# The hand-over from layer 1's attention to a 30-step recurrence: row factors through DRAM, two PSUM banks kept open, parameters made earlier

## The chip, the cores and the metric

The kernel runs on one core of one Trainium2 chip. TensorE (PE) multiplies matrices and transposes tiles, VectorE (DVE) and ScalarE (ACT) work element by element, GpSimd (POOL) does some elementwise work and issues gathers and scatters, SyncE (SP) issues transfers. The metric is the device time in microseconds (us) of the whole launch; lower is better.

## The reference, cut to what matters

Two layers work on 3327 nodes with 256 features. Each layer is a graph attention over a 0/1 adjacency matrix, then a feed-forward part. In layer 0 that part is a mixture of 16 experts, two for each node. In layer 1 it is a recurrence of 30 steps, each a small elementwise update, a layer norm and a 256x256 product. All is fp32.

```python
# layer 1, attention; x comes in layer-normed
wh = h @ W
wh1 = wh @ a[:F_OUT, :]
wh2 = wh @ a[F_OUT:, :]
e = wh1 + wh2.T
e = jnp.where(e > 0, e, ALPHA * e)
e = jnp.where(adj > 0, e, NEG_BIG)
attention = jax.nn.softmax(e, axis=-1)
h_prime = attention @ wh
return jax.nn.elu(h_prime)
...
# layer 1, recurrence: 30 times
h = h + 0.01 * jnp.tanh(h)
h = h * jax.nn.sigmoid(h)
h = _layernorm(h, ln_w, ln_b)
h = jnp.einsum('bsc,dc->bsd', h, W) + b
```

## The kernel before

The nodes stand in 26 tiles of 128 rows (NT = 26). The state x stays on chip. The program is written in one piece for all engines; a planner orders each engine's instructions by what they depend on and by when it expects them to be ready, so that an instruction can run well before its place in the text. An instruction handed to `keep_in_program_order` is held behind the instruction that was written before it for the same engine. Tiles come from pools: a pool with `bufs=2` gives each tile name two slots in turn, and pools that are closed make room for later ones. PSUM, where TensorE writes, has 8 banks of 512 fp32 in each of 128 partitions.

**Experts** (`work_off`, L797). 61 turns follow one another. A turn takes 128 gathered tokens through one expert's three matrices: products at L786 and L827, with weights that SP loads (L769 to L771) some turns ahead. PSUM banks come from `bank()`, a pool of four. Between the turns other pieces are slipped in by turn number: layer 1's parameters are loaded at turn 16 (L805), two preparations of the attention's weights come at turns 22 and 26 (L807, L809).

**Layer 1's attention** (`attend`, L201). Destination tiles are taken in nine parts, eight of three tiles and a last of two (`groups2`; its tiles are 24 and 25). For each part there are 26 steps j over source tiles. In a step ScalarE makes e (L252) from `rb`, VectorE makes the masked weights pT (L257), and TensorE adds to one accumulator for each destination tile (L262, 257 columns). `rb` holds the part's row factors: the vector `sc.row` of each of its tiles, laid along the free axis and repeated in every partition. `row_factors` (L214) makes it with one fp32 matmul for each tile (L221, two records each in the trace) into a PSUM bank of pool ps2, and ScalarE copies the bank (L225). The text asks for the next part's factors at step 13. When a part is done, VectorE reads its accumulators (L235 and L943 to L947, tile by tile), SP writes the result to DRAM (`kept`, L951), and VectorE normalizes the rows in place (L127); these pieces are mixed in among the next part's steps.

Two PSUM pools are open during the attention: ps2 with two slots named "bank", and ps2o with two slots for each of acc0, acc1 and acc2, six banks. Before the attention the same accumulators serve a projection; `spot` (L918) deals them out by a counter that starts at 0. Behind the attention stand the recurrence's parameters (L960 to L973): bb, a row vector, and wc, the 256x256 matrix with the layer norm's weight and mean worked in. They take four fp32 matmuls (eight records) and eight VectorE instructions.

**Recurrence** (L976 to L1046). The 26 tiles form seven groups, six of four and one of two. 30 steps of seven groups are taken in order, two groups to a pair, so that in 14 groups, two steps, seven pairs come: mostly 4+4, once 4+2 and once 2+4. For both groups of a pair `turn_group` (L992) runs first: tanh (L998), a sum on GpSimd (L1000), silu (L1001), statistics (L1005) and transposes into `pt` (L1008, two for each tile). Then `next_state` (L1012) runs for both: ScalarE copies `pt` to `zT` (L1019), in two pieces for the first group of a pair and in one for the second; TensorE multiplies by wc into `po` (L1024, two records for each matmul, 256 columns); VectorE scales and shifts into x (L1030). Transposes and products are held in program order. `pt` and `po` have two banks each and two slots each, eight banks, in pools ps3t and ps3o, which are opened when ps2 and ps2o are closed.

Of the kernel before, what the change touches and what calls it, by code (L numbers as in the profile page):

```python
# [20 lines left out]
P = 128  # L21
# [4 lines left out]
G = 4  # L26
# [4 lines left out]
def gat_moe_gat_recurrent_ffn(ctx: ExitStack, tc: tile.TileContext, a: dict, out: bass.AP):  # L31
# [169 lines left out]
    def attend(sc, wh, heads, row_groups, per_bank, finish, finished, pools, later, leave=False):  # L201
# [11 lines left out]

        def row_factors(ts, h):  # L214

            rb = rows_p.tile([P, most * P], F32, name="rb")
            for c0 in range(0, len(ts), 4):
# [25 lines left out]
        for k, (ts, h) in enumerate(parts):  # L243
# [4 lines left out]
            for j in range(NT):  # L248
                if j == NT // 2 and k + 1 < len(parts):
                    following = row_factors(*parts[k + 1])  # L250
# [107 lines left out]
    with ExitStack() as moe:  # L358
# [413 lines left out]

        def features_first(row):
# [23 lines left out]
        def work_off(s0, s1, aside):  # L797
# [3 lines left out]
            for s in range(s0, s1 + 1):  # L801
# [6 lines left out]
                if s == FIRST + 10:  # L808
                    without_mean(wv1, D + 2, ones_r, bank())  # L809
                hidT = made  # L810
# [80 lines left out]
    steps = ctx.enter_context(tc.tile_pool(name="steps", bufs=2))  # L891
    with ExitStack() as st:
# [7 lines left out]
        ps = st.enter_context(tc.tile_pool(name="ps2", bufs=2, space=PSUM))  # L900
# [15 lines left out]
        count = 0  # L916
# [39 lines left out]
        attend(sc, wh, 1, groups2, 1, add_elu, begin_state, (run, rows_p, ps, ps_o), deque())  # L956

        pb = ps.tile([P, 512], F32, name="bank")[:, :D]  # L960
        for k in range(KD):
            nc.tensor.matmul(
                pb, lhsT=lb[:, k : k + 1].to_broadcast([P, P]), rhs=fW[:, k, :], start=(k == 0), stop=(k == KD - 1)
            )
        nc.vector.tensor_tensor(bb, pb, fb, ALU.add)
        nc.vector.tensor_scalar(bb, bb, S, None, op0=ALU.mult)
        pc = ps.tile([P, 512], F32, name="bank")[:, :D]
        for k in range(KD):
            nc.vector.tensor_scalar(wc[:, k, :], fW[:, k, :], lw[:, k : k + 1], None, op0=ALU.mult)
            nc.tensor.matmul(pc, lhsT=ones_r, rhs=wc[:, k, :], start=(k == 0), stop=(k == KD - 1))  # L970
        for k in range(KD):
            nc.vector.scalar_tensor_tensor(wc[:, k, :], pc, -1.0 / D, wc[:, k, :], op0=ALU.mult, op1=ALU.add)
            nc.vector.tensor_scalar(wc[:, k, :], wc[:, k, :], S, None, op0=ALU.mult)  # L973


    with ExitStack() as st:  # L976
# [66 lines left out]
        for i in range(0, len(parts), 2):  # L1043
            two = [part + turn_group(part[1]) for part in parts[i : i + 2]]
            for part, pieces in zip(two, (2, 1)):
                next_state(*part, pieces)  # L1046
# [49 lines left out]
```

The softmax here doesn't subtract the row's maximum and nothing guards it: scores larger than these inputs give would overflow.

## Time and profile before

| what | us |
|---|---|
| three timed runs | 1965.48, 1968.25, 1968.59 (median 1968.25) |
| the profiled execution | 1964.56 |
| its span, first to last instruction | 1962.6 |
| layer 1's attention, first L262 to its last | 792.10 to 1091.83 |
| first transposes of the recurrence | 1094.32 |
| first L1024, last L1024's end | 1097.73, near 1955.5 |

A group's line in the profile names the line of the kernel, the engine, the operation and output<-input. "[2.49 <-DVE high L944]" at the end of a line says how long the engine was idle before it, and whose result ended that. Matmul ends are modelled, and some matmul records are missing, so idle time of TensorE is best read from starts. The chain of waits follows the last instruction back to what released it. SPq is SP's queue of transfers.

### The profile page before, as it was taken

Reading aid. Unit: us, or ns where it says so; the run is one execution under the profiler, and the core shown is the slowest. Engines: PE = TensorE matmul, PEld = TensorE weight load, DVE = VectorE, ACT = ScalarE, POOL = GpSimd, SP = SyncE. Lnnn points to the kernel's source line nnn. Section 1 sums busy time; section 2 is a strip of 40 time slices with the busy share of each in tenths; the row PEclk is TensorE's granted clock in tenths of the full one; section 3 lists DMA queues with packets and bytes.
Section 4 is the critical chain, followed back from the end, with each engine's and each line's share of the span. In section 5 each row is a group of like instructions: output and inputs, shape, how many; then the busy total and the mean of one; then the engine's idle time right before and its main releaser. Section 6 shows DMA issues by size and latency. Waiting matters only on the chain.

```text
span 1962.6 us, 33704 instructions
## 1 busy us (share of the span) xinstructions
PE 1908.9 (97%) x12032; PEld 1747.3 (89%) x12032; DVE 1281.6 (65%) x3827; ACT 1096.5 (56%) x1509; POOL 936.5 (48%) x864
## 2 busy tenths in 40 slices
PE   7999999999999997999999999999999999999998
PEld 6999999998999995888888888888888888888887
DVE  6887788832222225566767777777777777777778
ACT  2977766721111113666555666666666666666664
POOL 3020202353333322010000488878888887888886
PEclk9999999999999998999999999999999999999999
DMA  8978051099999874000000000000000000000003
GB/s 168 117 104 118 6 86 50 18 307 303 357 326 336 280 245 148 2 15 9 17 9 17 28 1 1 1 1 1 1 1 1 1 1 1 1 1 1 1 1 118
DMA packets 139756, 157.09 MB, mean 80 GB/s; under 512 B 52028, under 2 KB 99365, under 8 KB 139587
## 3 DMA queue, kind: packets, MB, share of 16 engines
q1 hardware_dynamic: 123466, 122.05, 20.1%
q0 software_dynamic: 11440, 28.09, 8.3%
q10 hardware_dynamic: 4680, 4.76, 0.7%
q8 instruction: 98, 1.61, 0.3%
q14 instruction: 72, 0.58, 0.1%
HBM read 164.58 MB, written 29.78 MB: 99 GB/s over the span
## 4 chain that ended last, share of the span: by engine, by line
PE 71%; issue 9%; POOL 5%; DVE 4%; DMA 3%; ACT 1%; SPq 0%; POOLq 0%; DVEq 0%; ACTq 0%
PE po L1024 35%; PE acc L262 24%; PE pt L1008 8%; POOL given L831 2%; DVE pT L257 2%; POOL rb L730 2%; DMA given<-wh,to 2%; PE bank L786 1%; PE bank L499 1%; DMA wh<-in_w_dram 1%; DMA lists<-pair,ati 1%; DVE x L913 1%; PE bank L221 0%; PE acc L162 0%; ACT zT L1019 0%
## 5 line engine op out<-in xcount | busy, mean ns | idle before, releaser
L1024 PE MATMUL po<-wc,zT 128*128 128x256 f32 x3120 | 700.3, 382 | 3.6 <-ACT zT L1019 3.6
L1024 PEld LDWEIGHTS po<-wc,zT 128*128 128x128 f32 x3120 | 583.0, 190 | 89.0 <-ACT zT L1019 11.2
L1000 POOL TENSOR_TENSOR th<-th,x 128x1024 f32<-128x1024 f32 (+1 forms) x210 | 460.8, 2216 | 120.7 <-ACT th L998 117.9
L252 ACT ACTIVATE e<-rb,minus,full 128x384 f32<-128x384 f32 (+3 forms) x494 | 400.5, 824 | 180.1 <-DVE pT L257 164.1
L257 DVE SCALAR_TENSOR_TENSOR pT<-e,part,adjT 128x384 f32<-128x384 f32 (+3 forms) x494 | 380.5, 774 | 137.5 <-PE acc L262 117.0
L1005 DVE BATCH_NORM_STATS2 stats<-z 128x6 f32<-128x256 f32 x780 | 275.1, 413 | 168.5 <-ACT z L1001 168.5
L1019 ACT COPY zT<-pt 128x512 f32<-128x512 f32 (+1 forms) x300 | 196.7, 721 | 294.1 <-PE pt L1008 294.1
L1030 DVE SCALAR_TENSOR_TENSOR x<-po,rr,bb 128x256 f32<-128x256 f32 x780 | 323.2, 475 | 48.7 <-PE po L1024 42.7
L262 PE MATMUL acc<-wh,pT 128*128 128x129 f32 x2704 | 310.1, 276 | 1.6 <-DVE pT L257 1.6
L262 PEld LDWEIGHTS acc<-wh,pT 128*128 128x128 f32 x2704 | 305.2, 192 | 2.0 <-DVE pT L257 2.0
L262 PE MATMUL acc<-s_wh,pT 128*128 128x257 f32 x1352 | 295.3, 380 | 0.8 <-DVE pT L257 0.7
L262 PEld LDWEIGHTS acc<-s_wh,pT 128*128 128x128 f32 x1352 | 255.9, 190 | 37.7 <-DVE pT L257 1.8
L120 POOL TENSOR_TENSOR rstd<-ve,neg_half 128x4 f32<-128x4 f32 (+3 forms) x28 | 30.4, 1086 | 415.1 <-DVE ve L118 331.5
L989 POOL TENSOR_TENSOR rr<-rr,neg_half 128x4 f32<-128x4 f32 (+1 forms) x210 | 207.2, 989 | 15.0
L1001 ACT ACTIVATE z<-th 128x1024 f32<-128x1024 f32 (+1 forms) x210 | 201.6, 1011 | 0.6 <-POOL th L1000 0.5
L998 ACT ACTIVATE th<-x 128x1024 f32<-128x1024 f32 (+1 forms) x210 | 198.4, 1002 | 0.9 <-DVE x L127 0.9
L1008 PE MATMUL pt<-ident,z 128*128 128x128 f32 x1560 | 189.1, 274 | 2.5 <-DVE high L944 2.5
L1008 PEld LDWEIGHTS pt<-ident,z 128*128 128x128 f32 x1560 | 178.6, 142 | 13.3 <-issue 2.9
L786 PEld LDWEIGHTS bank<-hT,wh 128*128 128x128 f32 x1280 | 149.1, 192 | 5.7 <-issue 3.7
L786 PE MATMUL bank<-hT,wh 128*128 128x128 f32 x1280 | 150.1, 275 | 3.4 <-DMA wh<-in_w_dram 3.4
L820 DVE TENSOR_TENSOR pT<-e,bank 128x512 f32<-128x512 f32 x61 | 41.9, 687 | 165.2 <-PE bank L786 165.1
L816 ACT ACTIVATE e<-bank 128x512 f32<-128x512 f32 x61 | 36.4, 597 | 196.7 <-PE bank L786 184.4
(189 smaller groups left out, 1333.5 us busy)
## 6 DMA issues: line engine op xcount, KB each, us to landing
wh<-in_w_dram SPq DMA_DIRECT2D x120, 512.0 KB
first_set<-in_w_dram SPq DMA_DIRECT2D x63, 512.0 KB
in_bytes<-in_adj_dram POOLq DMA_DIRECT2D x3, 2496.0 KB, 28.7
x<-in_x_dram SPq DMA_DIRECT2D x6, 512.0 KB
kept<-x SPq DMA_DIRECT2D x8, 384.0 KB
old<-kept SPq DMA_DIRECT2D x6, 512.0 KB
out_dram<-x SPq DMA_DIRECT2D x6, 512.0 KB
table_x<-row ACTq DMA_DIRECT2D x3, 768.0 KB
```

Of the source, the lines that this page charges most:

```text
L252: nc.scalar.activation(e[:, : n * P], rb[:, : n * P], AF.Relu, scale=sc.full[:, j, h : h + 1], bias=sc.minus[:, j, h : h + 1],)
L257: masked = nc.vector.scalar_tensor_tensor(pT[:, : n * P], e[:, : n * P], sc.part[:, j, h : h + 1], adjT[:, j // 2, ts[0] * P : (ts[-1] + 1 ...
L262: nc.tensor.matmul(po[c], lhsT=pT[:, c * P : (c + 1) * P], rhs=wh[:, j, h, :], start=(j == 0 and c % per_bank == 0), stop=(j == NT - 1), s ...
L786: nc.tensor.matmul(p[:, f, :], lhsT=w[:, k, f * P : (f + 1) * P], rhs=hT[:, k, :], start=(k == 0), stop=(k == KD - 1),)
L989: nc.gpsimd.tensor_tensor(r[:, :n], r[:, :n], neg_half[:, :n], ALU.pow)
L998: nc.scalar.activation(th[:, :n, :], hs, AF.Tanh, scale=1.0 / S)
L1000: nc.gpsimd.tensor_tensor(th[:, :n, :], th[:, :n, :], hs, ALU.add)
L1001: nc.scalar.activation(z[:, :n, :], th[:, :n, :], AF.Silu, scale=1.0 / S)
L1005: nc.vector.bn_stats(stats[:, j, :], z[:, j, :])
L1008: nc.tensor.transpose(pt[:, j, k, :], z[:, j, k * P : (k + 1) * P], ident)
L1024: nc.tensor.matmul(po[:, j, :], lhsT=zT[:, j, k, :], rhs=wc[:, k, :], start=(k == 0), stop=(k == KD - 1),)
L1030: nc.vector.scalar_tensor_tensor(x[:, ts[0] + j, :], po[:, j, :], rr[:, j : j + 1], bb, op0=ALU.mult, op1=ALU.add)
```

## The change

Four things change.

1. In layer 1's attention the row factors of all parts but the first are read from DRAM. At step 2 of the first part `put_factors` transposes `sc.row` once (26 rows of 128), VectorE copies that to SBUF, and SP writes it to a DRAM tile. `row_factors` then issues a read on SP that repeats the part's rows in all 128 partitions.
2. The pool ps2 is opened outside the attention's scope and stays open through the recurrence. `turn_group` takes its banks in turn from ps2 and from ps3t; each bank holds the transposes of two tiles, and `next_state` copies each bank by itself, for both groups of a pair. ps3t so has two banks instead of four.
3. The recurrence's parameters are made in the experts, at turn 30.
4. The counter of `spot` starts at 1, so that the accumulators' names are first used in the order acc2, acc0, acc1.

```diff
...
     quick = []
-    def attend(sc, wh, heads, row_groups, per_bank, finish, finished, pools, later, leave=False):
+    def attend(sc, wh, heads, row_groups, per_bank, finish, finished, pools, later, leave=False, spread=None):
...
         most = max(len(ts) for ts in row_groups)
         parts = [(ts, h) for ts in row_groups for h in range(heads)]
+        if spread:
+            queue, room = spread
+            factors = dram.tile([NT * heads, P], F32, name=f"factors{heads}")
+        def put_factors():
+            p = ps_r.tile([P, 512], F32, name="bank")[: NT * heads, :P]
+            nc.tensor.transpose(p, sc.row.rearrange("p t h -> p (t h)"), ident)
+            lines = room()[: NT * heads, :P]
+            nc.vector.tensor_copy(lines, p)
+            queue.dma_start(factors, lines)
         def row_factors(ts, h):
             rb = rows_p.tile([P, most * P], F32, name="rb")
+            if spread and (ts, h) != parts[0]:
+                here = factors[ts[0] * heads + h : ts[0] * heads + h + 1, :]
+                queue.dma_start(
+                    rb[:, : len(ts) * P].rearrange("p (c q) -> p c q", q=P),
+                    bass.AP(tensor=here.tensor, offset=here.offset, ap=[[0, P], [heads * P, len(ts)], [1, P]]),
+                )
+                return rb
             for c0 in range(0, len(ts), 4):
                 some = ts[c0 : c0 + 4]
                 p = ps_r.tile([P, 4, P], F32, name="bank")
...
             acc = [ps_o.tile([P, 512], F32, name=f"acc{q}") for q in range((n + per_bank - 1) // per_bank)]
             po = [acc[c // per_bank][:, (c % per_bank) * W : (c % per_bank + 1) * W] for c in range(n)]
             for j in range(NT):
+                if spread and j == 2 and k == 0:
+                    put_factors()
                 if j == NT // 2 and k + 1 < len(parts):
                     following = row_factors(*parts[k + 1])
                 e = work.tile([P, most * P], F32, name="e")
...
             nc.sync.dma_start(w2, a["w2"][bass.ds(e, 1)].rearrange("e (k p) h -> p (e k) h", p=P), **kw)
             behind = nc.sync.dma_start(w3, a["w3"][bass.ds(e, 1)].rearrange("e (f p) o -> p (e f) o", p=P), **kw).ins
+        def recurrence_parameters():
+            pb = bank()[:, :D]
+            for k in range(KD):
+                nc.tensor.matmul(
+                    pb, lhsT=lb[:, k : k + 1].to_broadcast([P, P]), rhs=fW[:, k, :], start=(k == 0), stop=(k == KD - 1)
+                )
+            nc.vector.tensor_tensor(bb, pb, fb, ALU.add)
+            nc.vector.tensor_scalar(bb, bb, S, None, op0=ALU.mult)
+            pc = bank()[:, :D]
+            for k in range(KD):
+                nc.vector.tensor_scalar(wc[:, k, :], fW[:, k, :], lw[:, k : k + 1], None, op0=ALU.mult)
+                nc.tensor.matmul(pc, lhsT=ones_r, rhs=wc[:, k, :], start=(k == 0), stop=(k == KD - 1))
+            for k in range(KD):
+                nc.vector.scalar_tensor_tensor(wc[:, k, :], pc, -1.0 / D, wc[:, k, :], op0=ALU.mult, op1=ALU.add)
+                nc.vector.tensor_scalar(wc[:, k, :], wc[:, k, :], S, None, op0=ALU.mult)
         def features_first(row):
             pt = ps_o.tile([P, 512], F32, name="acc0")[:, :D].rearrange("p (k q) -> p k q", k=KD)
             hT = turn.tile([P, 2, KD, P], F32, name="hT")[:, 0]
...
                     score_vectors()
                 if s == FIRST + 10:
                     without_mean(wv1, D + 2, ones_r, bank())
+                if s == FIRST + 14:
+                    recurrence_parameters()
                 hidT = made
                 if s < s1:
                     if s + 4 < s1:
...
     kept = dram.tile([NP, D], F32, name="kept")
     steps = ctx.enter_context(tc.tile_pool(name="steps", bufs=2))
+    ps = ctx.enter_context(tc.tile_pool(name="ps2", bufs=2, space=PSUM))
     with ExitStack() as st:
         keep = st.enter_context(tc.tile_pool(name="keep2", bufs=1))
...
         sc = Scores(keep, 1, s_wh[:, :, 0, 0:2].rearrange("p t (s h) -> p t s h", h=1))
         nc.vector.memset(wh[:, :, :, D : D + 1], 1.0)
         work = st.enter_context(tc.tile_pool(name="work2", bufs=2))
-        ps = st.enter_context(tc.tile_pool(name="ps2", bufs=2, space=PSUM))
         ps_o = st.enter_context(tc.tile_pool(name="ps2o", bufs=2, space=PSUM))
         names = cycle(("th", "z", "zT"))
...
                     nc.vector.tensor_tensor(here, here, two[k], ALU.add)
         add_results(groups1[:3])
-        count = 0
+        count = 1
         def spot():
             nonlocal count
...
             tiles = [x[:, t, :] for t in ts]
             normalized(tiles, tiles, S)
-        attend(sc, wh, 1, groups2, 1, add_elu, begin_state, (run, rows_p, ps, ps_o), deque())
-        pb = ps.tile([P, 512], F32, name="bank")[:, :D]
-        for k in range(KD):
-            nc.tensor.matmul(
-                pb, lhsT=lb[:, k : k + 1].to_broadcast([P, P]), rhs=fW[:, k, :], start=(k == 0), stop=(k == KD - 1)
-            )
-        nc.vector.tensor_tensor(bb, pb, fb, ALU.add)
-        nc.vector.tensor_scalar(bb, bb, S, None, op0=ALU.mult)
-        pc = ps.tile([P, 512], F32, name="bank")[:, :D]
-        for k in range(KD):
-            nc.vector.tensor_scalar(wc[:, k, :], fW[:, k, :], lw[:, k : k + 1], None, op0=ALU.mult)
-            nc.tensor.matmul(pc, lhsT=ones_r, rhs=wc[:, k, :], start=(k == 0), stop=(k == KD - 1))
-        for k in range(KD):
-            nc.vector.scalar_tensor_tensor(wc[:, k, :], pc, -1.0 / D, wc[:, k, :], op0=ALU.mult, op1=ALU.add)
-            nc.vector.tensor_scalar(wc[:, k, :], wc[:, k, :], S, None, op0=ALU.mult)
+        attend(
+            sc, wh, 1, groups2, 1, add_elu, begin_state, (run, rows_p, ps, ps_o), deque(),
+            spread=(nc.sync, lambda: fin.tile([P, D], F32, name="low")),
+        )
     with ExitStack() as st:
         ps_t = st.enter_context(tc.tile_pool(name="ps3t", bufs=2, space=PSUM))
+        turns = cycle((ps, ps_t))
         ps_o = st.enter_context(tc.tile_pool(name="ps3o", bufs=2, space=PSUM))
         last_p = st.enter_context(tc.tile_pool(name="last", bufs=2))
...
             nc.gpsimd.tensor_tensor(th[:, :n, :], th[:, :n, :], hs, ALU.add)
             nc.scalar.activation(z[:, :n, :], th[:, :n, :], AF.Silu, scale=1.0 / S)
             stats = small.tile([P, G, 6], F32, name="stats")
-            pt = ps_t.tile([P, G, KD, P], F32, name="pt")
+            pool = next(turns)
+            pt = [pool.tile([P, 2, KD, P], F32, name="bank") for _ in range(0, n, 2)]
             for j in range(n):
                 nc.vector.bn_stats(stats[:, j, :], z[:, j, :])
                 for k in range(KD):
                     tc.keep_in_program_order(
-                        nc.tensor.transpose(pt[:, j, k, :], z[:, j, k * P : (k + 1) * P], ident)
+                        nc.tensor.transpose(pt[j // 2][:, j % 2, k, :], z[:, j, k * P : (k + 1) * P], ident)
                     )
             return pt, stats
-        def next_state(step, ts, pt, stats, pieces):
+        def next_state(step, ts, pt, stats):
             n = len(ts)
             hs = x[:, ts[0] : ts[0] + n, :]
             rr = inv_norm(stats, n)
             zT = steps.tile([P, G, KD, P], F32, name="zT")
-            for c in range(0, n, G // pieces):
-                some = slice(c, min(c + G // pieces, n))
-                nc.scalar.copy(zT[:, some, :, :], pt[:, some, :, :])
+            for c in range(n // 2):
+                nc.scalar.copy(zT[:, 2 * c : 2 * c + 2, :, :], pt[c])
             po = ps_o.tile([P, G, D], F32, name="po")
             for j in range(n):
                 for k in range(KD):
...
                 move_pairs(out, hs, ts[0] // 2, (ts[-1] + 1) // 2, True)
         parts = [(step, ts) for step in range(N_STEPS) for ts in groups]
         for i in range(0, len(parts), 2):
             two = [part + turn_group(part[1]) for part in parts[i : i + 2]]
-            for part, pieces in zip(two, (2, 1)):
-                next_state(*part, pieces)
+            for part in two:
+                next_state(*part)
 # ---- launch: one core; inputs and outputs as the reference has them ----
```

## The prediction

> **What bounds the kernel now.** I read the page's engine shares and its chain of waits, then a table of three stretches, then the timeline at their seams.
>
> ```profile
> PE 1908.9 (97%) x12032; PEld 1747.3 (89%) x12032; DVE 1281.6 (65%) x3827; ACT 1096.5 (56%) x1509; POOL 936.5 (48%) x864
> ...
> PE 71%; issue 9%; POOL 5%; DVE 4%; DMA 3%; ACT 1%; SPq 0%; POOLq 0%; DVEq 0%; ACTq 0%
> ```
>
> TensorE carries the chain. Which part of the change counts depends on where TensorE's own stream has holes or spare instructions. The table's columns are stretch, length, busy time of each engine, clock, DMA share, GB/s:
>
> ```profile
> 792.10:1091.83 299.73, 299.36 (x1394) 261.71 (x1394) 201.28 (x457) 180.81 (x274) 19.39 (x16) 1.00 0.03 11
> 1091.83:1097.73 5.90, 3.41 (x17) 3.44 (x17) 4.20 (x14) 1.91 (x4) 0.70 (x1) 0.71 0.70 223
> 1097.73:1955.50 857.77, 854.13 (x4666) 758.06 (x4664) 639.36 (x2329) 562.06 (x713) 699.04 (x622) 1.00 0.02 7
> ```
>
> Layer 1's attention (first row) is TensorE without holes, so only instructions taken out of it count. The seam (second) and the recurrence (third) have holes. TensorE's timeline:
>
> ```profile
> 877.90 33.98 PE L262 MATMUL acc<-s_wh,pT 128*128 128x257 f32 x156
> 911.72 0.83 PE L221 MATMUL bank<-ident,row 128*128 128x128 f32 x6
> 912.39 33.98 PE L262 MATMUL acc<-s_wh,pT 128*128 128x257 f32 x156
> ...
> 1070.87 0.59 PE L962 MATMUL bank<-fW,lb 128*128 128x256 f32 x2
> ...
> 1094.32 3.58 PE L1008 MATMUL pt<-ident,z 128*128 128x128 f32 x16 [2.49 <-DVE high L944]
> 1097.73 7.07 PE L1024 MATMUL po<-wc,zT 128*128 128x256 f32 x32
> ```
>
> Row factors (L221) stand inside the attention: 0.67 us for six records (912.39-911.72); a matmul of 257 columns takes 33.81/156 = 0.217 us (the chain's figure for the same 156). At the seam TensorE idles 2.5 us for L944, VectorE's last read of tile 25's accumulator. In the recurrence I looked at three kinds of pair (4+2, 4+4, 2+4 tiles):
>
> ```profile
> 1146.22 1.47 PE L1008 MATMUL pt<-ident,z 128*128 128x128 f32 x12
> ...
> 1147.30 1.56 ACT L1019 COPY zT<-pt 128x512 f32<-128x512 f32 x3 [3.38 <-PE pt L1008]
> ...
> 1147.93 1.35 PE L1024 MATMUL po<-wc,zT 128*128 128x256 f32 x5 [0.24 <-ACT zT L1019]
> ```
>
> ```profile
> 1227.97 1.91 PE L1008 MATMUL pt<-ident,z 128*128 128x128 f32 x16
> ...
> 1229.04 1.07 ACT L1019 COPY zT<-pt 128x512 f32<-128x512 f32 x2 [3.37 <-PE pt L1008]
> ...
> 1229.72 0.45 PE L1024 MATMUL po<-wc,zT 128*128 128x256 f32 x1
> ```
>
> ```profile
> 1181.46 1.00 ACT L1019 COPY zT<-pt 128x1024 f32<-128x1024 f32 x1
> ...
> 1182.52 3.32 PEld L1024 LDWEIGHTS po<-wc,zT 128*128 128x128 f32 x16 [0.27 <-ACT zT L1019]
> ```
>
> In both first cases the copy starts 1.07 us after the first transpose: eight transposes (0.87 us at 0.109, the chain's 1.75 us for 16) and 0.2 of drain, although it reads only the first four. With 0.59 of copy and 0.08 of wait the matmul can start 1.75 us after the first transpose. Sixteen transposes last 1.75, so 4+4 just fits; twelve last 1.31, so 4+2 waits 0.4. In 2+4 a whole group's copy (1.00) comes late.
>
> **What the Trainium skill says.** "TensorE: Matmul & The Clock Gate" (Part 1, What's actually happening) gives half the clock after an idle window of some 3.4 us. The trace agrees in kind: after 2.5 us idle the 16 transposes took 0.224 us each, not 0.109, and the seam's clock reads 0.71. "PSUM — Partial Sum Buffer" (The four PSUM rules) says that DMA can't reach PSUM, so the transposed factors need a VectorE copy first; the trace shows no such transfer. "DMA: Bandwidth & Descriptors" (Anatomy of one DMA) gives 2.0 us plus bytes over 436 GB/s on GpSimd's path; a row-factor read of 128x384 fp32 is 197 KB, so my estimate is 2.5 us. The trace names no landing for SP's transfers; GpSimd's gathers land in 5.5 us, which I take as the upper end.
>
> **Edit 1, row factors.** The factors of attention parts 1 and 2 (counted from 0) were made at 789 to 791.5 beside ScalarE's chain to the first pT (792.10); taking them out gives nothing. Those of parts 3 to 8 stand in the full stream: five times 0.67 and once 0.45 = 3.8 us. The new transpose costs one record, 0.11. VectorE's copy of 26x128 is bounded by 0 (idle time before pT is 0.68 in each of 26 steps) and 0.3 (it waits its turn while pT queues behind it); I take 0. Saved: 3.7 us. Each of the eight transfers has 13 steps of 1.30 us = 17 us from issue to use, against 2.5 to 5.5, so none is waited for. ScalarE loses eight copies of 0.46, which bind nothing. On SP the read stands behind kept (L951) of the part before.
>
> **Edit 2, parameters.** Eight matmul records of 0.217 = 1.7 us leave the attention and enter the experts at turn 30. There TensorE waits for nothing between 480 and 715 us (its list of waits is empty; the chain's "issue" of 9% is records that are missing, 1280 of the 61x32 due at L786), and turns repeat every 5.52 us:
>
> ```profile
> 568.60 0.25 PEld L777 LDWEIGHTS acc<-ident,rb 128*128 128x128 f32 x2
> ...
> 574.12 0.25 PEld L777 LDWEIGHTS acc<-ident,rb 128*128 128x128 f32 x2
> ```
>
> They cost the same 1.7 us there. VectorE (25% busy there) hides its eight operations; a wait of the sum for wc costs 0 to 0.5, I take 0.1. Net: loss 0.1.
>
> **Edit 3, the seam.** Before, the last attention matmul starts near 1091.4 and the first L1024 at 1097.73: 6.3 us. Group 0's z was ready at 875.2 and the banks of the earlier row factors and parameters were read out by 1080.1, yet its transposes waited for L944 at 1094.17. I read this as a new PSUM pool waiting for every user of the pools on whose banks it lands. The kept pool has no such wait, so group 0's eight transposes follow the last matmul at once. They can't go earlier: program order pins them behind it. Group 1's eight and po still lie in new pools and wait for L944, 2.75 us after the last matmul. Then 0.87 us (full clock) to 1.8 (half), and L1024 starts after 3.7 to 4.6 us. Gain 1.7 to 2.6, I take 2.1. If those pools waited bank by bank, 16 transposes would follow at once and the gain were 6.3-1.75 = 4.5.
>
> **Edit 4, the recurrence.** 3120 matmuls of 0.218 and 1544 transposes of 0.109 make 848.5 us; the stretch has 857.8, so holes are 9.3, or 0.62 in each of 15 periods of two steps (57.3 us: 0.41 at 4+2, 0.15 at 2+4, the rest crumbs). Now each pair of tiles has its own bank and copy. A first copy can start after four transposes: 0.44+0.2+0.59+0.08 = 1.31 us, just what twelve last. The last hole shrinks because half a group's copy takes 0.59, not 1.00. I leave 0.09 per period: gain 8.0; ends 5 (ScalarE puts z, 1.06 us, before a copy) and 9.3. ScalarE pays 2x0.59-1.03 = 0.15 more per pair of 17.4 us; its share there is 66%, so this is hidden. Were it not, 105x0.15 = 16 us at most.
>
> **Sum.** -3.7+0.1-2.1-8.0 = -13.7 us. The profiled execution took 1964.56 (span 1962.6): 1950.9. The runs shown have a median of 1968.25, 3.7 above: 1954.5. I say 1954.
>
> **Rivals.**
> A, the forecast (0.64): 9 to 18 us less, 1950 to 1959 against the median.
> B, the recurrence's holes stay (0.15): copies start by when ScalarE is free, as at 2+4. Then -5.7, 1962.5. Against it: ScalarE idles 3.38 us before the copy at 4+2, so it is free there.
> C, new pools wait bank by bank (0.09): 2.4 more, 1952. Against it: the wait for L944 above.
> D, slower (0.12): SP's queue.
>
> ```profile
> SPq L951 <- DVE st L115: 273.0, 7, 66.5
> ```
>
> SP stands in kept's wait up to 66.5 us. If the read for part k+1 were issued behind kept of part k, which waits until 7.4 us into part k+1 (the timeline has kept's issue at 832.97, part 0's first reciprocal at 825.52), each of seven parts would start 7.4+2.5 = 9.9 us late: 69 us, about 2023. It decides when the read stands behind that kept. Against it: the text puts the read at step 13 of part k, kept of part k only in part k+1. Lesser mishaps of the same queue lie between.
>
> **How the numbers follow.** About 0.2% (3.9 us) is what a measurement of this kernel tells from no change. Faster: A, C and two thirds of B = 0.83; same: the rest of B = 0.05; slower: D = 0.12. The range runs from 1947, for full gains counted from the profiled run's lower base, to 1962, weaker seam and recurrence up to B. Outside are D and part of B.
>
> **What would show it.** L221 only before the first part and as one transpose; no hole before any L262; L962 to L973's work near 560 to 590 us. At the seam eight transposes straight after L262 and eight after L944. In the recurrence a copy 0.64 us after the first transpose and a period near 56.8 us. Wrong it would be with L252 waiting for a transfer into rb, with TensorE waiting in the experts, or with a period still at 57.3.

## The result and the profile after

| kernel | median, us | runs |
|---|---|---|
| before | 1968.42 | 4, of 1965.48 to 1970.27 |
| changed | 1950.54 | 4, of 1949.34 to 1954.65 |

The ratio is 0.9911, with a 95% interval of 0.9899 to 0.9922: 17.5 us less, between 15.4 and 19.9. The span of the profiled execution fell from 1962.6 to 1947.6. In the profile after, lines have moved: the attention's matmuls are L286 (before L262), its pT L281 (L257), the row factors' matmuls L243 (L221), their read L234 (new), the transposes of the recurrence L1040 (L1008), its products L1055 (L1024), the copies L1050 (L1019).

Engine shares and chain, from the page of the changed kernel:

```profile
PE 1897.3 (97%) x11987; PEld 1743.4 (90%) x11987; DVE 1279.9 (66%) x3828; ACT 1101.2 (57%) x1593; POOL 940.4 (48%) x864
...
PE 73%; issue 9%; POOL 5%; DVE 4%; DMA 2%; ACT 0%; SPq 0%; another core or an unknown queue 0%; POOLq 0%; DVEq 0%
```

TensorE still carries the chain; ScalarE has 84 instructions more: 90 copies of zT (390 of L1050, before 300 of L1019) and two loads of function tables more, eight copies of row factors fewer. The table of stretches of the changed kernel, with the columns of before:

```profile
796.93:1092.93 296.00, 294.68 (x1354) 256.44 (x1355) 200.07 (x451) 177.62 (x266) 19.79 (x16) 1.00 0.05 17
1092.93:1096.33 3.40, 1.78 (x18) 1.58 (x15) 2.83 (x9) 3.04 (x5) 0.00 (x0) 1.00 0.62 199
1096.33:1940.80 844.47, 844.47 (x4666) 757.19 (x4664) 638.18 (x2334) 569.04 (x805) 701.94 (x623) 1.00 0.02 7
```

In the third row TensorE's busy time is now the whole stretch; before, 3.6 us of it were idle. The length fell by much more, 13.3 us, so most of the saved time had stood inside the rows as "busy". The timeline of TensorE in the changed kernel:

```profile
794.01 0.83 PE L243 MATMUL bank<-ident,row 128*128 128x128 f32 x6
795.17 0.28 PE L224 MATMUL bank<-ident,row 128*26 128x128 f32 x1 [0.34 <-ACT row L196]
796.93 82.20 PE L286 MATMUL acc<-s_wh,pT 128*128 128x257 f32 x378 [1.47 <-DVE pT L281]
879.35 193.88 PE L286 MATMUL acc<-s_wh,pT 128*128 128x257 f32 x890 [0.23 <-DVE pT L281]
1073.94 2.00 PE L286 MATMUL acc<-s_wh,pT 128*128 128x257 f32 x8 [0.71 <-DVE pT L281]
1076.19 16.74 PE L286 MATMUL acc<-s_wh,pT 128*128 128x257 f32 x76 [0.25 <-DVE pT L281]
1092.77 1.04 PE L1040 MATMUL bank<-ident,z 128*128 128x128 f32 x8
1095.42 1.07 PE L1040 MATMUL bank<-ident,z 128*128 128x128 f32 x8 [1.61 <-DVE high L988]
1096.33 7.07 PE L1055 MATMUL po<-wc,zT 128*128 128x256 f32 x32
```

Row factors are gone from the stream (L243 only before the first part, L224 the one transpose), and between 879 and 1073 us nothing interrupts L286. Near 1074 us are holes that before did not have. At the seam eight transposes follow the last L286 at once and eight wait for VectorE, as forecast.

Every profile can be cut at the same instructions: attention (first to last start of its matmuls), seam (from there to the first product of the recurrence), recurrence (first to last start of the products). All in us, from one profile each; the last column is the timed ratio to the kernel before with its interval. The changed kernel was timed again as e9_after_again, and differs from the first row of it by 0.0005.

| kernel | attention | seam | recurrence | sum of the three | ratio |
|---|---|---|---|---|---|
| before | 299.36 | 6.28 | 857.60 | 1163.24 | 1 |
| changed | 295.63 | 3.77 | 844.09 | 1143.49 | 0.9911 (0.9899 to 0.9922) |
| e9_after_again | 295.76 | 3.77 | 844.09 | 1143.62 | 0.9916 (0.9903 to 0.9930) |
| e1_banks | 299.36 | 4.64 | 844.08 | 1148.08 | 0.9926 (0.9910 to 0.9943) |
| e2_pieces | 299.36 | 4.64 | 855.65 | 1159.65 | 0.9989 (0.9980 to 0.9998) |
| e3_rows | 295.45 | 5.93 | 857.91 | 1159.29 | 0.9982 (0.9975 to 0.9990) |
| e4_params | 299.36 | 4.65 | 857.59 | 1161.60 | 1.0010 (1.0001 to 1.0018) |
| e5_tile_waits | 295.67 | 1.96 | 845.50 | 1143.13 | 0.9918 (0.9904 to 0.9931) |
| e6_tile_count0 | 297.44 | 3.33 | 846.48 | 1147.25 | 0.9909 (0.9892 to 0.9926) |
| e7_params_back | 297.35 | 3.10 | 844.09 | 1144.54 | 0.9912 (0.9899 to 0.9926) |
| e8_both | 297.34 | 1.21 | 845.44 | 1143.99 | 0.9917 (0.9903 to 0.9930) |
| e10_late_reads | 311.63 | 3.77 | 844.07 | 1159.47 | 0.9988 (0.9981 to 0.9994) |

The three stages gave 19.8 us in the profile; the launch gained 17.5. Of the difference, 1.7 us is the time of the parameters in the experts (below). What is left, 0.6 us, lies inside the interval of the timed gain.

The sums rest on starts of matmuls. In these stretches no record is missing: the traces of both kernels have 1352 of the attention, 1560 transposes and 3120 products, as many as the program issues.

### The profile page after: what moved, and what is told of

The parts are those of the page before. It is cut to its first block, busy times and chain, and to the rows that moved or that the text cites. A ratio compares the mean times of both kernels' runs of the same rounds, so it can differ in the third digit from the quotient of the medians.

```text
span 1947.6 us, 33722 instructions
## 1 busy us (share of the span) xinstructions
PE 1897.3 (97%) x11987; PEld 1743.4 (90%) x11987; DVE 1279.9 (66%) x3828; ACT 1101.2 (57%) x1593; POOL 940.4 (48%) x864
## 3 DMA queue, kind: packets, MB, share of 16 engines
q8 instruction: 98, 1.61, 0.3%
## 4 chain that ended last, share of the span: by engine, by line
PE 73%; issue 9%; POOL 5%; DVE 4%; DMA 2%; ACT 0%; SPq 0%; another core or an unknown queue 0%; POOLq 0%; DVEq 0%
PE po L1055 35%; PE acc L286 24%; PE bank L1040 9%; DVE pT L281 2%; PE bank L828 2%; POOL given L875 2%; POOL rb L754 2%; DMA given<-wh,to 2%; PE acc L871 1%; PE bank L523 1%; PE acc L162 0%; DMA z<-given 0%; POOL rstd L120 0%; PE bank L147 0%; DMA th<-given 0%
## 5 line engine op out<-in xcount | busy, mean ns | idle before, releaser
L1055 PE MATMUL po<-wc,zT 128*128 128x256 f32 x3120 | 692.9, 380 | 0.0
L1055 PEld LDWEIGHTS po<-wc,zT 128*128 128x128 f32 x3120 | 584.5, 190 | 76.4
L1031 POOL TENSOR_TENSOR th<-th,x 128x1024 f32<-128x1024 f32 (+1 forms) x210 | 460.8, 2216 | 101.3 <-ACT th L1029 99.7
L281 DVE SCALAR_TENSOR_TENSOR pT<-e,part,adjT 128x384 f32<-128x384 f32 (+3 forms) x494 | 380.5, 774 | 134.2 <-PE acc L286 114.4
L1061 DVE SCALAR_TENSOR_TENSOR x<-po,rr,bb 128x256 f32<-128x256 f32 x780 | 321.0, 473 | 59.0 <-PE po L1055 57.3
L1050 ACT COPY zT<-bank 128x512 f32<-128x512 f32 x390 | 201.0, 598 | 269.9 <-PE bank L1040 269.9
L286 PE MATMUL acc<-wh,pT 128*128 128x129 f32 x2704 | 310.3, 276 | 1.6 <-DVE pT L281 1.6
L286 PEld LDWEIGHTS acc<-wh,pT 128*128 128x128 f32 x2704 | 305.2, 192 | 2.2 <-DVE pT L281 2.0
L286 PE MATMUL acc<-s_wh,pT 128*128 128x257 f32 x1352 | 294.7, 380 | 2.8 <-DVE pT L281 2.7
L286 PEld LDWEIGHTS acc<-s_wh,pT 128*128 128x128 f32 x1352 | 256.1, 190 | 41.1 <-DVE pT L281 5.2
L1020 POOL TENSOR_TENSOR rr<-rr,neg_half 128x4 f32<-128x4 f32 (+1 forms) x210 | 209.5, 997 | 17.5
L1040 PE MATMUL bank<-ident,z 128*128 128x128 f32 x1560 | 187.7, 273 | 1.6 <-DVE high L988 1.6
L1040 PEld LDWEIGHTS bank<-ident,z 128*128 128x128 f32 x1560 | 177.0, 141 | 12.4 <-ACT zT L1050 1.8
```

The costliest lines, as they stand in the source:

```text
L281: masked = nc.vector.scalar_tensor_tensor(pT[:, : n * P], e[:, : n * P], sc.part[:, j, h : h + 1], adjT[:, j // 2, ts[0] * P : (ts[-1] + 1 ...
L286: nc.tensor.matmul(po[c], lhsT=pT[:, c * P : (c + 1) * P], rhs=wh[:, j, h, :], start=(j == 0 and c % per_bank == 0), stop=(j == NT - 1), s ...
L1020: nc.gpsimd.tensor_tensor(r[:, :n], r[:, :n], neg_half[:, :n], ALU.pow)
L1031: nc.gpsimd.tensor_tensor(th[:, :n, :], th[:, :n, :], hs, ALU.add)
L1040: nc.tensor.transpose(pt[j // 2][:, j % 2, k, :], z[:, j, k * P : (k + 1) * P], ident)
L1050: nc.scalar.copy(zT[:, 2 * c : 2 * c + 2, :, :], pt[c])
```

## The experiments

### The recurrence: smaller PSUM tiles, or shorter copies

e1_banks is the kernel before with the new PSUM tiles of two tiles of nodes each, in a new pool of four banks: nothing is kept open, no row factors, no parameters.

```diff
-        ps_t = st.enter_context(tc.tile_pool(name="ps3t", bufs=2, space=PSUM))
+        ps_t = st.enter_context(tc.tile_pool(name="ps3t", bufs=4, space=PSUM))
...
-            pt = ps_t.tile([P, G, KD, P], F32, name="pt")
+            pt = [ps_t.tile([P, 2, KD, P], F32, name="bank") for _ in range(0, n, 2)]
...
-            for c in range(0, n, G // pieces):
-                some = slice(c, min(c + G // pieces, n))
-                nc.scalar.copy(zT[:, some, :, :], pt[:, some, :, :])
+            for c in range(n // 2):
+                nc.scalar.copy(zT[:, 2 * c : 2 * c + 2, :, :], pt[c])
```

> The kernel before with one thing of the change: each pair of tiles has its own PSUM bank and its own copy, in one new pool of four banks; row factors, parameters and the seam as before. Theory (a copy waits for all transposes of its PSUM tile, so smaller tiles let it start after four): from the first L1024 to the last, 857.6 us before and 844.1 in the changed kernel, this run shows 843 to 846; the seam stays at 6.3 us; the whole is about 13 us faster. Rival (the gain needs the pool that is kept open and the turns between two pools): the stretch stays above 854.

e2_pieces leaves the PSUM tile as it was and copies the second group in two pieces too.

```diff
-            for part, pieces in zip(two, (2, 1)):
+            for part, pieces in zip(two, (2, 2)):
```

> The kernel before, with the second group of a pair copied in two pieces like the first, from PSUM tiles that still hold four node tiles. Theory (the PSUM tile decides when a copy may start): the waits of 0.40 us at 4+2 and of 0.07 us at each 4+4 stay, only those at 2+4 go, so the recurrence stretch falls from 857.6 to 854 to 856. Rival (the long copy of the second group is what costs): it falls below 848.

e1_banks has the changed kernel's recurrence to 0.01 us (844.08), e2_pieces has 855.65. Timeline of e2_pieces, first a 4+2 pair, then a 4+4 pair:

```profile
1150.66 1.47 PE L1008 MATMUL pt<-ident,z 128*128 128x128 f32 x12
...
1151.73 1.56 ACT L1019 COPY zT<-pt 128x512 f32<-128x512 f32 x3 [3.31 <-PE pt L1008]
...
1152.37 3.94 PE L1024 MATMUL po<-wc,zT 128*128 128x256 f32 x17 [0.24 <-ACT zT L1019]
...
1223.55 1.91 PE L1008 MATMUL pt<-ident,z 128*128 128x128 f32 x16
...
1224.62 2.05 ACT L1019 COPY zT<-pt 128x512 f32<-128x512 f32 x4 [2.88 <-PE pt L1008]
```

The same two kinds in the changed kernel:

```profile
1144.42 1.47 PE L1040 MATMUL bank<-ident,z 128*128 128x128 f32 x12
...
1145.06 1.56 ACT L1050 COPY zT<-bank 128x512 f32<-128x512 f32 x3 [3.24 <-PE bank L1040]
...
1145.73 2.61 PE L1055 MATMUL po<-wc,zT 128*128 128x256 f32 x11
...
1159.63 1.91 PE L1040 MATMUL bank<-ident,z 128*128 128x128 f32 x16
...
1160.27 2.05 ACT L1050 COPY zT<-bank 128x512 f32<-128x512 f32 x4 [2.82 <-PE bank L1040]
```

With the same copies of 512 columns, the first one starts 1.07 us after the first transpose in e2_pieces and 0.64 us in the changed kernel. So the wait for eight transposes belongs to the PSUM tile, not to what the copy reads: here a copy of half a tile waits for all that is written to the tile. In the 4+2 pair the product follows 1.71 us after the first transpose with the large tile and 1.31 us with the small ones, exactly when twelve transposes are over. What e2_pieces gains, 1.95 us, comes from the 2+4 pairs alone: from first transpose to first transpose such a pair takes 6.56 us instead of 6.69, fifteen times. The bank kept open isn't needed for any of this, since e1_banks has none. The seam of e1_banks, expected at 6.3 us, was 4.64; why is told under Edit 3.

### The attention: row factors, and where the parameters stand

e3_rows is the kernel before with the row factors' way through DRAM alone (`spread`, `put_factors` and the read in `row_factors`, as in the change's diff). e4_params is the kernel before with the parameters' code moved to turn 30 and nothing else.

```diff
                     without_mean(wv1, D + 2, ones_r, bank())
+                if s == FIRST + 14:
+                    recurrence_parameters()
```

> The kernel before, with the row factors of layer 1's parts 1 to 8 read from DRAM; parameters and recurrence as before. From the first L262 of layer 1 to the last: 299.35 us before, 295.63 in the changed kernel. Theory (the row factors' matmuls stood in a full TensorE stream, the parameters' did not): 295.3 to 296.0, the changed kernel's whole gain there. Rival (the prediction's step: row factors 3.7, parameters 1.7 of an expected 5.4, and something new costs 1.7): 295.3 to 296.0 here too, but then e4_params must show 297.6. No wait of L252 for a transfer.

> The kernel before, with the recurrence's parameters made at the experts' turn 30; row factors and recurrence as before. Theory (eight matmul records of 1.73 us filled a hole where VectorE closes part 7 while a step of the last part lasts only 0.87 us): layer 1's attention stays at 298.9 to 299.4 us and the hole opens near 1070 us, while the experts' turn 30 gets 1.7 us longer, so the move loses 1.3 to 1.8 us. Rival (the prediction's step, the attention's stream is full): the attention falls to 297.6 and the move is even.

e3_rows gave 3.9 us in the attention. In it the planner also moved the parameters' eight records ahead of the first L286; what such a move gives by itself is the subject of e4_params. e4_params took eight records out of the attention, and its length stayed 299.36 us. Timeline of TensorE in e4_params:

```profile
1058.01 21.64 PE L262 MATMUL acc<-s_wh,pT 128*128 128x257 f32 x98
1080.36 2.00 PE L262 MATMUL acc<-s_wh,pT 128*128 128x257 f32 x8 [0.71 <-DVE pT L257]
1082.60 16.74 PE L262 MATMUL acc<-s_wh,pT 128*128 128x257 f32 x76 [0.24 <-DVE pT L257]
```

Counted from starts, at 0.216 us for a record: 98 records from 1058.01 end at 1079.18, 1.18 before the next one; eight more from 1080.36 end at 1082.09, 0.51 before the next. Together 1.7 us, the time of the eight records that were moved away. Here the last part has two tiles, so a step lasts 4 x 0.216 = 0.87 us, while VectorE closes the part before. The chain of waits of the changed kernel (start, length, instruction) shows it there:

```profile
1067.48 0.48 DVE pT L281
...
1069.68 0.40 DVE pT L281
1070.07 0.33 DVE x L991
...
1076.19 16.32 PE acc L286 x74
```

From 1067.4 to 1076.2 us the chain runs through VectorE: pT in turn with the close of part 7 (L991 is its last addition). The parameters' matmuls had stood in time in which TensorE would have waited for it.

Moved into the experts they cost their full time. Timeline of TensorE in the changed kernel, around the turn that they join:

```profile
567.36 0.38 PE L819 MATMUL acc<-ident,rb 128*128 128x128 f32 x2
...
572.88 0.38 PE L819 MATMUL acc<-ident,rb 128*128 128x128 f32 x2
...
574.83 1.03 PE L802 MATMUL bank<-fW,lb 128*128 128x256 f32 x4
575.69 1.03 PE L810 MATMUL bank<-wc,ones_r 128*128 128x256 f32 x4
576.55 3.62 PE L828 MATMUL bank<-hT,first_set 128*128 128x128 f32 x31
```

A turn lasts 5.52 us (572.88 - 567.36). In this one the next products begin at 576.55, 1.72 us after L802 began: the turn is 7.25 us long, and VectorE's eight operations add nothing to it. For e4_params this means about 1.7 us lost in the experts and none won in the attention; it was timed 2.0 us slower than before (0.2 to 3.5).

e7_params_back is the changed kernel with the parameters' code behind the attention again, as before the change.

```diff
-                if s == FIRST + 14:
-                    recurrence_parameters()
```

> The changed kernel, with the recurrence's parameters written again behind the attention instead of in the experts. The planner now puts their matmuls before the first L262 of layer 1, where TensorE waits 1.5 us for the first pT, since a bank of the kept pool is free. Theory (eight records of 1.73 us cost their length in the experts' full stream and nothing in a wait): the experts' turn 30 is 1.7 us shorter, the stretch from the last experts' matmul to the first L262 grows by 0 to 0.5, so 1 to 2 us are won against the changed kernel, less 0.2 to 0.9 for group 0's transposes, which now stand before the last steps of the attention. Rival (what is won is given back by VectorE's eight operations at the attention's start): no difference, or slower.

The planner put the eight matmuls ahead of the first L286, into the 1.47 us in which TensorE waits for the first pT, where they are nearly free (in e3_rows they stand there too). But it also put group 0's eight transposes into the attention, which grew to 297.35, and the seam shrank to 3.10. (The transposes are held only behind the instruction written before them, which presumably is one of the moved matmuls now.) The three stages lost 1.05 us, and the experts won 1.7: the turn of 7.25 us is back at 5.52. The whole can't be told from the changed kernel, so the 1 to 2 us that were expected did not show.

### The seam: pools that wait bank by bank

e5_tile_waits is the changed kernel with the new PSUM pools of the recurrence waiting for each of their banks' last users alone. e8_both is e5_tile_waits and e7_params_back together. e6_tile_count0 is e5_tile_waits with the accumulators' counter back at 0 (two pools wait bank by bank in it, not three as its expectation says).

```diff
-        ps_t = st.enter_context(tc.tile_pool(name="ps3t", bufs=2, space=PSUM))
+        ps_t = st.enter_context(tc.tile_pool(name="ps3t", bufs=2, space=PSUM, reuse_waits="tile"))
...
-        ps_o = st.enter_context(tc.tile_pool(name="ps3o", bufs=2, space=PSUM))
+        ps_o = st.enter_context(tc.tile_pool(name="ps3o", bufs=2, space=PSUM, reuse_waits="tile"))
```

> The changed kernel, with the two new PSUM pools of the recurrence told to wait bank by bank for earlier tiles in the same bank, instead of for every user of the pools they land on. Theory (what is left of the seam is the wait of group 1's transposes and of po for the last read of tile 25): sixteen transposes follow the last L262 at once, po waits only for tile 24's reads, and from the last L262 to the first L1055 there are 1.9 to 2.3 us instead of 3.77; the whole is some 1.7 us faster than the changed kernel. Rival (ScalarE's copies, held up by tile 24's exponential, set the start): the seam stays above 3 us.

> The changed kernel with the three pools of the recurrence's start waiting bank by bank, as in e5_tile_waits, and the accumulators' counter back at 0. Theory: the counter decides which of the last part's accumulators the recurrence's banks land on; with 0 the second bank of group 1 lands on one that VectorE reads late, so its four transposes wait about 1.5 us and the seam is about 3.4 us instead of 1.96. Rival: all sixteen transposes run at once as in e5_tile_waits, seam 1.9 to 2.0. The whole differs from the changed kernel by less than 2 us either way.

> The changed kernel with both: parameters behind the attention in the text, and new pools that wait bank by bank. Theory: the gains add, about 3 us below the changed kernel, near 1947; from the last L262 to the first L1055 there are 1.1 to 2.3 us. Rival: they overlap, since group 0's transposes have left the seam already, and the gain is that of one alone, about 1.7 us.

In e5_tile_waits all sixteen transposes follow the last L286 and the seam falls to 1.96, as expected. So the wait of group 1 for VectorE at the seam (1.61 us in the changed kernel) comes from how a new pool waits, as the prediction read it. The launch gains nothing. Timeline of e5_tile_waits:

```profile
1096.11 1.91 PE L1040 MATMUL bank<-ident,z 128*128 128x128 f32 x16
...
1098.00 1.28 ACT L1032 ACT_TABLE_LOAD   x1
...
1099.29 1.06 ACT L1032 ACTIVATE z<-th 128x1024 f32<-128x1024 f32 x1
1100.37 1.28 ACT L989 ACT_TABLE_LOAD   x1
...
1101.66 0.42 ACT L989 ACTIVATE low<-low 127x256 f32<-127x256 f32 x1
...
1101.98 1.05 ACT L1050 COPY zT<-bank 128x512 f32<-128x512 f32 x2
...
1102.61 3.72 PE L1055 MATMUL po<-wc,zT 128*128 128x256 f32 x16 [1.13 <-ACT zT L1050]
```

The copies of the second group stand on ScalarE behind two loads of function tables (1.28 us each), a z and tile 25's exponential, so the products wait for ScalarE instead. In both kernels these copies start 6.1 us after the last attention matmul. In e6_tile_count0 the counter does what its theory said: twelve transposes at once, four 1.2 us later behind VectorE, seam 3.33. But then TensorE waits 2.14 us for VectorE's L1061, 14 us behind the first product. VectorE is late there because of two L127, which normalize rows of x in place. They first wait 1.21 us for the write of kept and then take 1.87 and 2.45 us, beside GpSimd's L1031 (1100.01 to 1104.74). In the changed kernel they are over before that L1031 begins and take 0.40 us each. One profile doesn't show whether the counter has a part in this. In e8_both TensorE waits 1.04 us for VectorE about 10 us behind the first product. So in each of the three profiles a later wait (1.13, 1.04 or 2.14 us) took back part or all of what the seam gained. The sums of the three stages of changed, e5_tile_waits and e8_both lie within 0.9 us, and no timed ratio leaves the changed kernel's interval. The gains of 1.7 and 3 us that were expected of e5_tile_waits and e8_both did not come. With the pools' common wait as it is in the change, the counter's start was not tried.

### The price of a transfer that nothing hides

e10_late_reads is the changed kernel with each part's read made to wait for the last pT of the part before.

```diff
-                if j == NT // 2 and k + 1 < len(parts):
+                if not spread and j == NT // 2 and k + 1 < len(parts):
...
+            if spread and k + 1 < len(parts):
+                following = row_factors(*parts[k + 1], masked.ins)
```

> The changed kernel, but the read of the next part's row factors is written behind the last step of a part and waits for that part's last pT; nothing else changes. It prices a transfer that nothing hides, which is what my rival D (slower) rests on. A stall of TensorE per part is the transfer's time from issue to use, plus e (0.71 us) and pT (0.62), less what TensorE still has queued when the last pT is ready (about two steps of 1.30, less the 0.7 that pT trails: 1.9), so the transfer's time less about 0.5. Theory (transfer 2.5 us, as the estimate in the prediction): 8 stalls of 2.0, attention 295.6 to about 312 us, ratio to the changed kernel about 1.008. Rival (5.5 us, like GpSimd's gathers): 8 stalls of 5.0, attention about 336, ratio about 1.02. Rival D's own figure is another 7.4 us per part, which only a read behind the wait of kept would add; here the queue is not behind it.

Timeline of e10_late_reads at the end of the first part (its pT is L286, e L281, the products L291):

```profile
828.30 0.62 DVE L286 SCALAR_TENSOR_TENSOR pT<-e,part,adjT 128x384 f32<-128x384 f32 x1 [0.68 <-PE acc L291]
828.95 0.36 SPq L234 DMA_DIRECT2D rb<-factors  x1
...
832.21 1.90 ACT L281 ACTIVATE e<-rb,minus,full 128x384 f32<-128x384 f32 x3 [6.44 <-DMA rb<-factors]
...
833.62 0.70 PE L291 MATMUL acc<-s_wh,pT 128*128 128x257 f32 x2 [1.52 <-DVE pT L286]
```

From issue to ScalarE's start is 3.26 us, and 3.0 to 3.3 at the parts behind it: between the two bounds of the forecast, nearer the lower. From the start of part 1 to that of part 8 a part lasts 35.68 us on average, against 33.95 in the changed kernel: 1.7 us for each transfer. The expectation's rule, the transfer's time less 0.5, would give 2.7. TensorE had more in hand than it counted: part 0's products began until 831.7, 2.8 us after that last pT. The attention is 16 us longer, of which 1.7 are a half clock at its start (below). That the expected 312 us came out (311.63) is therefore luck: the transfer was longer than 2.5 us, the stall shorter than 2.0, and the clock made up the difference. All of the row factors' gain, and most of the recurrence's, would be gone.

In the changed kernel the queue of SP shows why none of this is paid:

```profile
795.90 0.39 SPq L227 DMA_DIRECT2D factors<-low  x1
797.27 27.75 SPq L234 DMA_DIRECT2D rb<-factors  x2
837.79 0.37 SPq L995 DMA_DIRECT2D kept<-x  x1
858.51 0.32 SPq L234 DMA_DIRECT2D rb<-factors  x1
```

The read for part 2 is issued at 824.70, right behind part 0's last e (823.97, 0.71 long), which frees its slot of `rb`; part 2's own first e starts at 859.08, 34 us later. The kept of part 0 follows the read. The planner put the reads earlier than the text does, and no e waits for a transfer.

## Why the prediction was right, point by point

The forecast was 1954 with a sum of -13.7; measured were 1950.5 and -17.5. Two of its four terms had the wrong size, in opposite directions (5.5 us too little for the recurrence, 1.6 us too much for the parameters), and a third depends on the execution. That the sum came this near is in part luck.

| term | forecast | measured in profiles |
|---|---|---|
| Edit 1, row factors | -3.7 | -3.7 to -3.9 |
| Edit 2, parameters | -1.7 and +1.8 | 0 and +1.7 |
| Edit 3, seam | -2.1 | -2.5, or -0.9 where the old seam runs at full clock |
| Edit 4, recurrence | -8.0 | -13.5 |

**Edit 1** held with its working: six records out of each of five full parts and four out of one, no transfer waited for, the copy on VectorE free (part 0 lasts 33.92 us before and 33.91 after). The factors of parts 1 and 2 gave nothing, as said: where they stood, TensorE now waits 1.47 us for the first pT instead of 0.46.

**Edit 2** failed at "eight matmul records of 0.217 = 1.7 us leave the attention". The sum took the attention as a stream without holes because its row of the table read 299.36 of 299.73 busy. It was full there because the planner had put these very records where TensorE would have waited for VectorE. Taken out, they left the wait (e4_params). The other half, 1.7 us in the experts, was right. So the edit loses 1.7 us where the forecast had 0.1. One reading beside it was wrong too: no records are missing at L786. All 61 x 32 = 1952 are in the trace, 1280 that read wh and 672 that read first_set; what the chain's "issue" stands for there stays open. That the experts' stream is full rests on the turn of 5.52 us that became 7.25. The whole stage of the experts can't show that: with the same code in it, it lasts 349.2 us in the profile of e6_tile_count0 and 355.2 in that of e9_after_again.

**Edit 3** went as said: group 0 at once, group 1 behind VectorE. The first L1055 starts 3.77 us after the last attention matmul, inside the 3.7 to 4.6 of the forecast, with the transposes at full clock. What was not seen is that the old seam itself has two lengths, 6.28 and 5.93 (before, e3_rows) or 4.64 (e1_banks, e2_pieces, e4_params), by whether its sixteen transposes ran at half clock. How often each happens in timed runs wasn't measured. Nor was the kept pool run alone: that it lets group 0 go at once is read from the changed kernel beside e1_banks, where all sixteen transposes go into a new pool and wait 2.5 us. Rival C (new pools wait bank by bank) did not hold: group 1 waited 1.61 us for VectorE's L988. It was priced 2.4 us better. e5_tile_waits made it so, and 1.4 of the 1.8 us that the seam gained came back as a wait for ScalarE: the price left out what is late next.

**Edit 4** was right in its mechanism and too small. The failing term is "3120 matmuls of 0.218". That is the 6.98 us of a 4+4 pair, from its first product to the next pair's first transpose, over 32 records. Such a pair wasn't full, as its rows show, before and in the changed kernel:

```profile
1220.99 7.14 PE L1024 MATMUL po<-wc,zT 128*128 128x256 f32 x32
1227.97 1.91 PE L1008 MATMUL pt<-ident,z 128*128 128x128 f32 x16
```

```profile
1161.38 7.07 PE L1055 MATMUL po<-wc,zT 128*128 128x256 f32 x32
1168.29 1.91 PE L1040 MATMUL bank<-ident,z 128*128 128x128 f32 x16
```

From row to row it is 6.98 against 6.91 us. The second record of such a pair's products starts 0.286 us after the first, in the changed kernel 0.218. The first weight load (PEld), which reads the copy, starts only 0.04 us before the first product (1225.26 and 1225.30 in e2_pieces, whose 4+4 pairs last as long as those of before), and the second load is late with it; in the changed kernel the lead is 0.10 us (1161.28 and 1161.38). The timeline can't print this wait: a product's modelled length, 0.38 us, is longer than the step to the next one, and waits below 0.15 us are merged into one row. At 0.216 the work of the recurrence is 3120 x 0.216 + 1544 x 0.109 = 842 us. That leaves 15.4 us of holes before, not 9.3, and 1.9 after. "4+4 just fits" was the same error: it missed by 0.07 us, 75 times.

From first transpose to first transpose a 4+2 pair fell from 7.00 to 6.56 us, a 2+4 pair from 6.69 to 6.56 and a 4+4 pair from 8.72 to 8.66 (by 0.068). By number of pairs that is 6.5, 2.0 and 5.1 us. The first two are what the prediction saw (0.41 and 0.15 for each two steps); the third it had among "crumbs". Two steps now take 56.4 us (from the twelve transposes at 1144.42 to those at 1200.82), against 57.3 before and 56.8 expected. The "pair of 17.4 us" beside ScalarE's extra work is two pairs; the work was hidden all the same, since 1.9 us of holes are all that is left.

The sum over the profiles is -3.7 + 1.7 - 2.5 - 13.5 = -18.0, against -17.5 measured. The single edits, timed alone, give -14.6 (e1_banks, its quicker seam included), -3.5 and +2.0, together -16.1; the other 1.4 are within their intervals, so no gain of the kept pool could be shown by time, only the shorter seam in the trace.

**Rivals.** B (holes stay) fell with the third row of the table. D (the queue of SP) fell with the order of the queue: read, then kept of the part before. Its other half, an unhidden transfer of 2.5 to 5.5 us, is now priced at 1.7 us for each of eight parts.

## What to carry to other kernels

A row of many matmuls that reads as busy may hide a wait in every group: compare the steps from start to start with the shortest that occurs, before a mean is used as the price. Before work is taken out of a stream that looks full, ask what the engine would wait for without it; work that fills a wait is free there and costs its full time where it is put. In this kernel a PSUM tile was handed on as a whole. Where that is so, the tile should be no larger than the piece that the next engine is meant to begin with.

## What the hardware showed that had not been expected

A pause of TensorE is followed by half clock in some executions and not in others, at the same place. After 2.5 us at the old seam two of five profiles had it. The hole at the start of the attention, 1.47 us behind one of 0.34, was left at half clock in two (e6_tile_count0, e10_late_reads) of the five profiles that have it. Stretches of 1 us in e6_tile_count0 (columns as in the tables of stretches, the clock third from the right):

```profile
792.00:793.00 1.00, 0.96 (x3) 0.78 (x4) 1.00 (x2) 1.00 (x2) 0.00 (x0) 0.57 0.00 0
793.00:794.00 1.00, 1.00 (x4) 0.82 (x3) 0.18 (x1) 1.00 (x3) 0.00 (x0) 0.50 0.21 81
794.00:795.00 1.00, 1.00 (x4) 0.81 (x3) 0.00 (x0) 0.33 (x1) 0.00 (x0) 0.50 0.33 115
795.00:796.00 1.00, 1.00 (x5) 0.76 (x5) 0.62 (x1) 0.33 (x1) 0.00 (x0) 0.72 0.00 0
```

The low clock lasts 3.4 us (from 792.14 to 795.55) and costs 1.7, which is why this attention is 297.44 us and not 295.7.

The traces' record of the granted clock gives an order to this. In each of the twelve profiles all changes of the clock lie whole multiples of 3.413 us apart. TensorE's busy share in the interval of that length just before tells the two outcomes apart, at each of the two places:

| place | busy share, half clock follows | busy share, full clock stays |
|---|---|---|
| old seam | 28% (before), 27% (e3_rows) | 43 to 46% (e4_params, e2_pieces, e1_banks) |
| hole at the attention's start | 47% (e6_tile_count0, e10_late_reads) | 49% (e9_after_again), 51% (changed), 69 and 78% (e5_tile_waits, where two intervals share the pause) |

So the same pause costs 1.3 to 1.7 us more, or nothing more, and this goes with how much idle time falls into one interval. That is an order in ten cases, not a rule that was tested: at the hole the two sides lie close together, the shares rest on modelled ends of matmuls, no single threshold fits both places (43% kept the clock at one, 47% lost it at the other), and no run moved the intervals on purpose. Near 195 us three other profiles (e1_banks, e9_after_again, e10_late_reads) have half clock after intervals that were 61 to 67% busy.

The Trainium skill ("TensorE: Matmul & The Clock Gate", Part 1, What's actually happening) lets the clock fall after an idle window of some 3.4 us and calls the window free-running, so that the moment varies from run to run. The traces agree with the window, its length and its running free. They do not show that a whole window must be idle: pauses of 1.5 to 2.5 us were enough, in windows that were 27 to 47% busy.

The hole came with the change: before it, row factors stood there, and in e3_rows and e7_params_back the parameters filled it.
